# Factorization kernel: order of accumulating transfers, W loads, bias additions and x sums

## Chip, cores and metric

One NeuronCore of a Trainium2 chip runs the whole program. The metric is device time in microseconds (us); lower is better. A core has five engines that run side by side, each through its own program in order: TensorE (PE, with its weight loads listed as PEld), VectorE (DVE), ScalarE (ACT), GpSimd (POOL) and SyncE (SP). They meet through semaphores. DMA transfers are issued here by SP (loads, stores) and by GpSimd (transfers that add to their destination).

## The reference

`x` is 1024 x 512, `weight` is 64 embeddings x 512 x 512, all float32:

```python
out_lin = x @ lin_w.T + lin_b
xv = jnp.einsum('bf,efm->bem', x, weight)
zp = jnp.einsum('bf,efm->bem', jnp.square(x), jnp.square(weight))
interaction = 0.5 * jnp.sum(jnp.square(xv) - zp, axis=1)
return out_lin + interaction
```

The sum over embeddings of `zp` is `square(x)` times the sum of `square(W)`, one product. What stays is `x @ W` for 64 embeddings, squared and summed.

## The kernel before

**Tiling.** The embeddings go through in 16 groups of four (`q`). One group is a product of `x` with four matrices, done by Strassen's method in Winograd's form at two levels: 7 outer products (`i` of "1", "2", "6", "7", "5", "3", "4", in this order) of 7 inner products each, and each for two halves `j` of the rows. That is 98 products a group, each of a 128x128 operand with 128x512 columns. W is held in four tiles `WB[kk][v]`: `kk` is a half of the contraction, `v` a pair of embeddings; one tile is 1 MB.

**Operands.** The x operands of all 49 combinations are made once, at the start, into `xs` by `outer_x` and `inner_x` (L154 to L185: two outer and four inner sums for each outer product). The W operands are made in every group on GpSimd: `outer_t` (L380, sums of whole tiles into `T5`, `T6` or `WB[0][0]`) and `inner_t`, which makes three tiles for each outer product: `tp` (L391, 128x1024), `t6` (L393) and `t4` (L395, both 128x512). They feed the inner products "5" and "7", "6", and "4".

**Results.** Each pair (outer product, `j`) is a `unit` with three PSUM banks `x`, `v`, `y`. ScalarE copies `x` into `y` (L475), after which `y` is added to; VectorE combines the banks with earlier results into `z` tiles (L446, L457, L458, L467), GpSimd does `rest` (L472). When a quarter of the output is complete in `z`, ScalarE squares it in place (`squares`, L497), and `gather` (L506) adds it to the accumulators `acc[0]` (in the profile acc_69) or `acc[1]` (acc_70) in SBUF by an accumulating DMA on GpSimd's queue. A gather to the same part of an accumulator waits for the gather before it to land. The names "c", "a", "b" tell which third of the results a gather carries; "c" to r=1 and "a" go in four transfers of 512 KB, (j=0, u=0), (1, 0), (0, 1), (1, 1), the others in two of 1 MB.

**Squares of W.** `w_squares` (L510) squares two halves of W tiles into `w2_sb` on ScalarE (L515), then an accumulating DMA of 1 MB adds `w2_sb` to `w2_sum` (L522): four times a group. There is one `w2_sb`.

**Order.** Nothing is scheduled by a tool. Every step is put into a `Stream` with a number `t`; the steps are sorted by it and issued in this order, so `t` fixes only the order within each engine's program. It isn't a time at which something starts. One unit of `t` is about one product, and a group covers 98:

```python
for _, _, fn in sorted(self.items, key=lambda v: v[:2]):
    fn()
```

Units start at `g0 + 14*n + 7*j`, with `g0 = 98*q`, and their inner products "1", "5", "6", "2", "7", "3", "4" stand at +0, +2, +4, +6, +8, +10, +12. Consecutive units overlap, so the product at `t` is product number t - 3 of its group (counted from the 98*q-th product). For instance "4" of unit (1, j=0), at t = 12, is number 9 and reads `t4` of outer product "1"; "6" of unit (2, j=0), at 18, is number 15 and reads `t6` of "2"; "6" of unit (4, j=0), at 88, is number 85.

**What the change touches.** L354: places of the bias additions `add_bias` (L348, one 128x512 VectorE operation for each of eight accumulator parts, in groups 1 to 4). L538: order of the four W loads of the next group on SP's queue (L358). L543 to L557: places of `outer_t` and `inner_t`. L567 and L568: places of gathers. L580: place of the first W squares of a group; L521: how far their accumulating transfer stands behind them. L596: the x sums of outer product "7". L758: a sum of squared x (`last_sx`, L628) for the last product.

Of the kernel before, what the change touches and what calls it, by code (L numbers as in the profile page):

```python
# [28 lines left out]
def kernel(  # L29
# [31 lines left out]
    nc = tc.nc  # L61
# [45 lines left out]
    def xsl(i, o):  # L107
        return xs[:, SLOT[i], SLOT[o], :]

    st = Stream()  # L110
# [35 lines left out]
    def quarter(r, kk, n):  # L146

        w = slice(0, 3) if n is None else n
        for i, rk in BLOCK.items():
            if rk == (r, kk):  # L150
                return a21[i] if n == 3 else xs[:, SLOT[i], w, :]
        return A21[:, w, :]

    def outer_x(i, eng=nc.vector):  # L154
        if i in BLOCK:
            return []

        def put(n):
            w = slice(0, 3) if n is None else n

            def of(o):
                return a21[o] if n == 3 else xs[:, SLOT[o], w, :]

            def src(r, kk):
                return quarter(r, kk, n)

            if i == "5":
                eng.tensor_add(of(i), src(1, 0), src(1, 1))
            elif i == "6":
                eng.tensor_sub(of(i), of("5"), src(0, 0))  # L170
            elif i == "7":
                eng.tensor_sub(of(i), src(0, 0), src(1, 0))
            else:
                eng.tensor_sub(of(i), src(0, 1), of("6"))

        return [lambda: put(None), lambda: put(3)]

    def inner_x(i, eng=nc.vector):
        add, sub = eng.tensor_add, eng.tensor_sub
        return [  # L180
            lambda: add(xsl(i, "5"), a21[i], xsl(i, "4")),
            lambda: sub(xsl(i, "6"), xsl(i, "5"), xsl(i, "1")),
            lambda: sub(xsl(i, "7"), xsl(i, "1"), a21[i]),
            lambda: sub(xsl(i, "3"), xsl(i, "2"), xsl(i, "6")),
        ]  # L185
# [160 lines left out]
    def add_bias(r, j, s):  # L346
        o = acc[r][:, j, s]
        nc.vector.scalar_tensor_tensor(o, bias, 2.0, o, ALU.mult, ALU.add)  # L348
# [1 line left out]
    st.at(-1, lambda: nc.sync.dma_start(bias, lin_b.partition_broadcast(P)))  # L350

    for n in range(4):
        for r, t in enumerate((22.6, 36.6)):
            st.at(98 * (n + 1) + t, lambda r=r, n=n: add_bias(r, n // 2, n % 2))  # L354

    def load_w(q, kk, v):
        src = weight[4 * q + 2 * v : 4 * q + 2 * v + 2]
        nc.sync.dma_start(  # L358
            WB[kk][v], src.rearrange("u (p k) m -> p u k m", k=NK)[:, :, ts(kk, 2)]
        )  # L360
# [12 lines left out]
    def outer_t(i, u):  # L373
        a, b = {
            "5": (WB[0][1], WB[0][0]),
            "6": (WB[1][1], T5),
            "7": (WB[1][1], WB[0][1]),
            "4": (WB[1][0], T6),
        }[i]
        nc.gpsimd.tensor_sub(OUTER[i][:, u], a[:, u], b[:, u])  # L380
# [3 lines left out]
    def inner_t(q, i, n):  # L384

        b = OUTER[i]
        k = 2 if n == "tp" else 1
        t = tpool.tile([P, k, M], F32, tag=n, name=f"{n}_{q}_{i}")
        TI[q, i, n] = t
        if n == "tp":  # L390
            nc.gpsimd.tensor_sub(t, b[:, 1], b[:, :, 0])  # L391
        elif n == "t6":
            nc.gpsimd.tensor_sub(t[:, 0], b[:, 1, 1], TI[q, i, "tp"][:, 0])  # L393
        else:
            nc.gpsimd.tensor_sub(t[:, 0], b[:, 0, 1], TI[q, i, "t6"][:, 0])  # L395
# [96 lines left out]
    def squares(t, q, n, j, wait):  # L492
        z = place(q, n)
        for u in range(2):
            st.at(
                t + max(wait, 0.1) * u,
                lambda u=u: nc.scalar.activation(z[:, u, j], z[:, u, j], AF.Square),  # L497
            )
# [3 lines left out]
    def gather(t, q, n, r, j, u):  # L502
        def fn():
            z = place(q, n)[:, u]
            o, z = (acc[r], z) if j is None else (acc[r][:, j], z[:, j])
            nc.gpsimd.dma_start(o, z, accum_op=ALU.add)  # L506

        st.at(t, fn)

    def w_squares(t, q, v, u):  # L510
        first = q == v == u == 0

        def sq(kk):
            o = (w2_sum if first else w2_sb)[:, ts(kk, 2)]
            nc.scalar.activation(o, WB[kk][v][:, u], AF.Square)  # L515

        for kk in range(2):
            st.at(t + 0.1 * kk, lambda kk=kk: sq(kk))
        if not first:
            st.at(  # L520
                t + 5,  # L521
                lambda: nc.gpsimd.dma_start(w2_sum, w2_sb, accum_op=ALU.add),  # L522
            )

# [10 lines left out]
    for q in range(NQ):  # L535
        g0 = 98 * q
        last = q == NQ - 1
        for kk, v, t in ((1, 0, -41), (0, 1, -39), (0, 0, -37), (1, 1, -10)):  # L538
            if q:
                st.at(g0 + t, lambda q=q, kk=kk, v=v: load_w(q, kk, v))  # L540

        for i, t0, t1 in (
            ("5", -8, 2) if q else ("5", -11, -10.9),  # L543
            ("6", 14.2, 14.3) if q else ("6", 0.5, 0.6),
            ("7", 28.7, 28.8),
            ("4", 50, 53),
        ):
            for u, t in enumerate((t0, t1)):
                st.at(g0 + t, lambda i=i, u=u: outer_t(i, u))
        for i, *times in (  # L550
            ("1", -4.3, -0.6, 2.1) if q else ("1", -11.5, -11.4, -11.3),
            ("2", 6.4, 10.1, 10.2) if q else ("2", -5, -4.9, -4.8),
            ("6", 20.7, 20.8, 27),
            ("7", 34.4, 34.5, 39.7),
            ("5", 43.1, 43.2, 43.3),
            ("3", 57.9, 58, 61.7),
            ("4", 81, 81.1, 81.2),  # L557
        ):
            for n, t in zip(("tp", "t6", "t4"), times):
                st.at(g0 + t, lambda q=q, i=i, n=n: inner_t(q, i, n))  # L560
        for n, (i, (addend, dst)) in enumerate(UNITS.items()):
            for j in range(2):
                unit(g0 + 14 * n + 7 * j, q, i, j, addend, dst)

        for k, n, r, times in (
            (1, "c", 0, ((None, 38.8), (None, 52.9))),
            (4, "c", 1, ((0, 73), (0, 87), (1, 80), (1, 92.8))),  # L567
            (5, "a", 0, ((0, 88), (0, 99.5), (1, 96.5), (1, 107.2))),  # L568
            (6, "b", 1, ((None, 111.3), (None, 124.2))),
        ):  # L570
            for j in range(2):
                t = g0 + 14 * k + 7 * j + 14.6
                squares(t - (0.95 if last and n == "b" else 0), q, n, j, 4 * (k == 4))
            for m, (j, t) in enumerate(times):
                if not last or n == "c":
                    gather(g0 + t, q, n, r, j, m % 2)
        if q == 0:
            w_times = (-6, 14.8, 37, 56.6)
        else:
            w_times = (-15, 14.8, 37, 56.6)  # L580
        for n, t in enumerate(w_times):
            w_squares(g0 + t, q, n // 2, n % 2)
    for kk, v in ((0, 0), (1, 0), (0, 1), (1, 1)):
# [3 lines left out]
    for sums, t in (  # L587
# [5 lines left out]
    ):  # L593
        for n, fn in enumerate(sums):
            st.at(t + 0.1 * n, fn)
    for n, fn in enumerate(outer_x("7") + inner_x("7")):  # L596
        st.at(7.6 + 1.1 * n, fn)
    for n, fn in enumerate(outer_x("3", nc.gpsimd) + inner_x("3", nc.gpsimd)):
        st.at(36.9 + 0.1 * n, fn)

# [10 lines left out]
    def square_xq(r, kk):  # L613
        nc.scalar.activation(XQ[r][:, kk], XQ[r][:, kk], AF.Square)
# [7 lines left out]
    def last_sx(i):  # L622
        t = WB[0][0] if i in "56" else T5
        t = t.rearrange("p u l (n q) -> p u (l n) q", q=Q)
        SX[i] = t[:, "5673".index(i) % 2]
        a21, a22 = XQ[1][:, 0], XQ[1][:, 1]
        if i == "5":
            nc.gpsimd.tensor_add(SX[i], a21, a22)  # L628
        elif i == "6":
            nc.gpsimd.tensor_sub(SX[i], SX["5"], last_x("1"))  # L630
        elif i == "7":
            nc.gpsimd.tensor_sub(SX[i], last_x("1"), a21)
        else:
            nc.gpsimd.tensor_sub(SX[i], last_x("2"), SX["6"])
# [120 lines left out]
        st.at(g + t, lambda r=r: load_xq(r))  # L755
    for t, r, kk in ((-28, 1, 0), (-27.9, 1, 1), (-25, 0, 0), (-24.9, 0, 1)):
        st.at(g + t, lambda r=r, kk=kk: square_xq(r, kk))
    for i, t in zip("5673", (-24.1, -9.9, -9, -5)):  # L758
        st.at(g + t, lambda i=i: last_sx(i))
    for i, t in zip("5674", (-9.8, -9.7, -8.9, -4.9)):  # L760
        st.at(g + t, lambda i=i: last_tw(i))
# [71 lines left out]
```

## Time and profile before

| | us |
|---|---|
| runs: median of 3 (lowest to highest) | 1413.41 (1413.05 to 1416.66) |
| the profiled execution | 1413.1 |
| its span, first to last instruction | 1411.2 |
| busy: TensorE | 1402.8 |
| busy: GpSimd | 1244.5 |
| busy: VectorE | 883.1 |
| busy: ScalarE | 623.2 |
| one group of 98 products, groups 1 to 14 (first weight load to first weight load in the trace) | 84.1 to 85.2 |

So 1.9 us of the profiled execution lie outside its span, and it is 0.3 us below the median. The granted TensorE clock is 1.00 throughout. TensorE's row must be read with care: matmuls are pipelined and their ends are modelled, so short stalls don't show in it. The weight loads (PEld) start evenly, two for each product; where two starts lie further apart, TensorE stood still.

### The profile page before, as it was taken

What the parts mean: (1) busy time and instruction counts of PE and PEld (TensorE: products, weight loads), DVE (VectorE), ACT (ScalarE), POOL (GpSimd) and SP (SyncE); (2) the same over time, 40 slices, a digit from 0 to 9 for tenths busy, and PEclk for the clock granted to TensorE, in tenths of its full rate; (3) what the DMA queues carried; (4) which work ended last, traced back from release to release, by engine and by line L of the source; (5) the groups of instructions that cost most, each with busy time, mean ns of one, the idle gap of its engine ahead of it and who ended that gap; (6) DMA issues with size and microseconds to landing.
All of it is one profiled execution on the core that took longest, in us unless ns stands there. A gap on an engine that the chain in (4) does not pass through costs nothing.

```text
span 1411.2 us, 11148 instructions
## 1 busy us (share of the span) xinstructions
PE 1402.8 (99%) x3340; PEld 633.7 (45%) x3340; DVE 883.1 (63%) x1277; ACT 623.2 (44%) x824; POOL 1244.5 (88%) x806
## 2 busy tenths in 40 slices
PE   9999999999999999999999999999999999999999
PEld 5444444444444444444444444444444444444446
DVE  6765657657576565656656566565656656566565
ACT  3344353453534444352453535444352453535443
POOL 7788989888898888989998899888989989899894
PEclk9999999999999999999999999999999999999999
DMA  5299898999989899898999989889898989989876
GB/s 216 52 216 208 190 212 167 225 189 220 189 177 223 167 220 208 191 212 162 235 181 225 192 182 219 172 213 202 192 209 170 230 178 229 188 181 224 169 179 142
DMA packets 58108, 273.63 MB, mean 194 GB/s; under 512 B 5440, under 2 KB 8000, under 8 KB 41792
## 3 DMA queue, kind: packets, MB, share of 16 engines
q0 software_dynamic: 36432, 198.20, 71.6%
q1 hardware_dynamic: 21328, 74.19, 15.1%
q10 hardware_dynamic: 288, 0.52, 0.1%
q8 instruction: 27, 0.44, 0.1%
q14 instruction: 33, 0.27, 0.0%
HBM read 72.61 MB, written 2.10 MB: 53 GB/s over the span
## 4 chain that ended last, share of the span: by engine, by line
PE 80%; POOL 9%; DMA 8%; issue 2%; DVE 1%; ACT 0%; POOLq 0%; ACTq 0%; DVEq 0%
PE y L421 33%; PE v L421 22%; PE x L421 21%; DMA acc<-z 5%; DMA w<-weight 3%; POOL t L380 2%; POOL tp L391 2%; POOL z L472 1%; POOL t L393 1%; PE lin L216 1%; POOL acc L506 1%; POOL t L395 1%; PE y_last L660 1%; POOL w_sum L522 1%; PE x_last L660 0%
## 5 line engine op out<-in xcount | busy, mean ns | idle before, releaser
L421 PE MATMUL y<-t,xs 128*128 128x512 f32 x896 | 422.0, 593 | 3.3 <-DVE z L467 1.8
L475 ACT COPY y<-x 128x512 f32<-128x512 f32 x224 | 127.8, 570 | 573.7 <-PE x L421 573.5
L467 DVE TENSOR_TENSOR z<-y,s 128x512 f32<-128x512 f32 x192 | 132.8, 692 | 237.1 <-PE y L421 236.0
L497 ACT ACTIVATE z<-z 128x1024 f32<-128x1024 f32 x256 | 260.2, 1054 | 22.7 <-POOL z L472 20.2
L421 PEld LDWEIGHTS y<-t,xs 128*128 128x128 f32 x896 | 169.5, 190 | 219.7 <-issue 209.8
L506 POOL DMA_DIRECT2D acc<-z x190 | 196.4, 1056 | 68.9 <-DMA acc<-z 33.2
L421 PE MATMUL x<-w,xs 128*128 128x512 f32 x512 | 248.4, 592 | 0.0
L421 PE MATMUL y<-tp,xs 128*128 128x512 f32 x448 | 229.3, 593 | 0.7 <-DVE s L446 0.6
L421 PE MATMUL v<-tp,xs 128*128 128x512 f32 x448 | 228.9, 592 | 0.4 <-POOL tp L391 0.4
L472 POOL TENSOR_TENSOR z<-z,s 128x1024 f32<-128x1024 f32 x64 | 149.9, 2364 | 46.3 <-DVE s L467 46.3
L421 PE MATMUL x<-t,xs 128*128 128x512 f32 x384 | 188.3, 592 | 0.0
L391 POOL TENSOR_TENSOR tp<-w 128x1024 f32<-128x1024 f32 x64 | 175.5, 2743 | 4.1 <-PE y L421 2.9
L467 DVE TENSOR_TENSOR z<-v,s 128x512 f32<-128x512 f32 x192 | 132.7, 691 | 71.0 <-PE v L421 69.2
L458 DVE TENSOR_TENSOR z<-y,z 128x512 f32<-128x512 f32 x192 | 132.4, 690 | 55.8 <-PE y L421 55.6
L380 POOL TENSOR_TENSOR t<-w,t 128x1024 f32<-128x1024 f32 x64 | 159.3, 2567 | 0.0
L458 DVE TENSOR_TENSOR z<-x,z 128x512 f32<-128x512 f32 x192 | 132.3, 689 | 35.8 <-PE x L421 34.3
L421 PEld LDWEIGHTS x<-w,xs 128*128 128x128 f32 x512 | 97.3, 190 | 122.0 <-issue 121.3
L515 ACT ACTIVATE w_sb<-w 128x1024 f32<-128x1024 f32 x126 | 126.0, 1050 | 28.0 <-DMA w<-weight 23.5
L391 POOL TENSOR_TENSOR tp<-t 128x1024 f32<-128x1024 f32 x48 | 137.1, 2855 | 0.0
L421 PEld LDWEIGHTS y<-tp,xs 128*128 128x128 f32 x448 | 84.7, 190 | 109.0 <-issue 103.8
L421 PEld LDWEIGHTS v<-tp,xs 128*128 128x128 f32 x448 | 85.0, 190 | 107.9 <-issue 103.4
L421 PE MATMUL v<-w,xs 128*128 128x512 f32 x256 | 130.7, 592 | 0.0
(113 smaller groups left out, 1448.3 us busy)
## 6 DMA issues: line engine op xcount, KB each, us to landing
w<-weight SPq DMA_DIRECT2D x64, 1024.0 KB, 11.2
acc<-z POOLq DMA_DIRECT2D x128, 512.0 KB, 8.6
w_sum<-w_sb POOLq DMA_DIRECT2D x63, 1024.0 KB, 12.3
acc<-z POOLq DMA_DIRECT2D x62, 1024.0 KB, 7.6
w<-x SPq DMA_DIRECT2D x2, 1024.0 KB, 10.3
out<-z SPq DMA_DIRECT2D x7, 256.0 KB, 2.3
xs<-x SPq DMA_DIRECT2D x2, 384.0 KB, 7.0
t<-lin_wT ACTq DMA_DIRECT2D x2, 256.0 KB, 3.8
```

The costliest lines, as they stand in the source:

```text
L216: nc.tensor.matmul(LIN[n], quarter(0, kk, (0, 1, 3, 2)[2 * s + l])[:, ts(j, P)], lw_sb[:, 2 * kk + l, :], start=(kk == 0 and l == 0), stop ...
L380: nc.gpsimd.tensor_sub(OUTER[i][:, u], a[:, u], b[:, u])
L391: nc.gpsimd.tensor_sub(t, b[:, 1], b[:, :, 0])
L393: nc.gpsimd.tensor_sub(t[:, 0], b[:, 1, 1], TI[q, i, "tp"][:, 0])
L421: nc.tensor.matmul(d[bank], xsl(i, o)[:, ts(j, P)], operand_b(q, i, o), start=start, stop=True, skip_group_check=True,)
L458: nc.vector.tensor_add(zblk(q, dst, j, b), d[bank], zblk(q, addend, j, b))
L467: nc.vector.tensor_add(s if both else zblk(q, dst, j, b), d[bank], s)
L472: nc.gpsimd.tensor_add(place(q, n)[:, 1, j], place(q, src)[:, 1, j], d["s"])
L475: st.at(t0 + 0.5, lambda: nc.scalar.copy(d["y"], d["x"]))
L497: lambda u=u: nc.scalar.activation(z[:, u, j], z[:, u, j], AF.Square),
L506: nc.gpsimd.dma_start(o, z, accum_op=ALU.add)
L515: nc.scalar.activation(o, WB[kk][v][:, u], AF.Square)
```

## The change

Four kinds of edits:

- two bias additions a group (groups 1 to 4) stand 5 places later;
- on SP, W tile (0, 0) is loaded second and (0, 1) third, instead of the reverse; the load of (1, 1) gets another number;
- the first W squares of a group stand 4.2 places earlier, and with them the accumulating transfer to `w2_sum`; a smaller distance (3.2 instead of 5) is written for t < 0; some gathers and W sums stand at other places;
- the x sums of outer product "7" are made by GpSimd before its first `outer_t("6")`, not by VectorE among the first units; `last_sx("5")` stands 10.1 places later.

No operation is added or removed.

```diff
     for n in range(4):
-        for r, t in enumerate((22.6, 36.6)):
+        for r, t in enumerate((27.6, 41.6)):
             st.at(98 * (n + 1) + t, lambda r=r, n=n: add_bias(r, n // 2, n % 2))
...
             st.at(
-                t + 5,
+                t + (3.2 if t < 0 else 5),
                 lambda: nc.gpsimd.dma_start(w2_sum, w2_sb, accum_op=ALU.add),
             )
...
-        for kk, v, t in ((1, 0, -41), (0, 1, -39), (0, 0, -37), (1, 1, -10)):
+        for kk, v, t in ((1, 0, -41), (0, 0, -37.5), (0, 1, -37), (1, 1, -3)):
...
-            ("5", -8, 2) if q else ("5", -11, -10.9),
+            ("5", -9.9, 2) if q else ("5", -11, -10.9),
...
-            ("1", -4.3, -0.6, 2.1) if q else ("1", -11.5, -11.4, -11.3),
-            ("2", 6.4, 10.1, 10.2) if q else ("2", -5, -4.9, -4.8),
+            ("1", -6.4, -1.4, 2.1) if q else ("1", -11.5, -11.4, -11.3),
+            ("2", 6.4, 6.5, 10.2) if q else ("2", -5, -4.9, -4.8),
...
-            ("4", 81, 81.1, 81.2),
+            ("4", 81, 82.1, 84.1),
...
-            (4, "c", 1, ((0, 73), (0, 87), (1, 80), (1, 92.8))),
-            (5, "a", 0, ((0, 88), (0, 99.5), (1, 96.5), (1, 107.2))),
+            (4, "c", 1, ((0, 73), (0, 84), (1, 80), (1, 91.5))),
+            (5, "a", 0, ((0, 88), (0, 99.5), (1, 96.5), (1, 110.3))),
...
-            w_times = (-15, 14.8, 37, 56.6)
+            w_times = (-19.2, 14.8, 37, 56.6)
...
-    for n, fn in enumerate(outer_x("7") + inner_x("7")):
-        st.at(7.6 + 1.1 * n, fn)
-    for n, fn in enumerate(outer_x("3", nc.gpsimd) + inner_x("3", nc.gpsimd)):
-        st.at(36.9 + 0.1 * n, fn)
+    for i, t in (("7", -4.7), ("3", 36.9)):
+        for n, fn in enumerate(outer_x(i, nc.gpsimd) + inner_x(i, nc.gpsimd)):
+            st.at(t + 0.1 * n, fn)
...
-    for i, t in zip("5673", (-24.1, -9.9, -9, -5)):
+    for i, t in zip("5673", (-14, -9.9, -9, -5)):
         st.at(g + t, lambda i=i: last_sx(i))
```

The order on GpSimd around the start of a group becomes, with the order of before under it:

```
after:  tp4 t6_4 WSUM c(0,1) t4_4 a(0,0) outer5 c(1,1) tp1 a(1,0) t6_1 a(0,1) outer5 t4_1 tp2 t6_2 t4_2 a(1,1) b outer6
before: tp4 t6_4 t4_4 c(0,1) a(0,0) WSUM outer5 c(1,1) tp1 a(1,0) t6_1 a(0,1) outer5 t4_1 tp2 a(1,1) t6_2 t4_2 b outer6
```

Here `t6_2` is the tile `t6` of outer product "2", `a(0,1)` the gather of "a" for j=0, u=1, and WSUM the accumulating transfer to `w2_sum`. On ScalarE the two W squares now stand between the two squares of "c" for j=1, instead of behind both.

## The prediction, made before the run

> **What bounds the kernel now.** I read the page first, for the engines and queues.
>
> ```profile
> PE 1402.8 (99%) x3340; PEld 633.7 (45%) x3340; DVE 883.1 (63%) x1277; ACT 623.2 (44%) x824; POOL 1244.5 (88%) x806
> ...
> q0 software_dynamic: 36432, 198.20, 71.6%
> q1 hardware_dynamic: 21328, 74.19, 15.1%
> ```
>
> TensorE is the bound, and the DMA engines (87% over both queues) and GpSimd (88%) are close behind: a reordering can win only what TensorE loses in stalls, and it must not run into the other two. So I went through the weight loads in order of time. Two loads start 0.43 us apart when nothing stalls. From 26 us on, 20 distances exceed 0.5 us; what they have above 0.43 each sums to 12.98 us. Five kinds make it up, and each is shown once.
>
> Kind 1, the bias. The timelines of weight loads and of VectorE, group 1:
>
> ```profile
> 151.14 0.30 PEld L421 LDWEIGHTS y<-tp,xs 128*128 128x128 f32 x2 [1.03 <-DVE s L446]
> ...
> 148.06 1.24 DVE L348 SCALAR_TENSOR_TENSOR acc<-bias,acc 128x512 f32<-128x512 f32 x1 [1.54 <-DMA acc<-z]
> 149.22 0.68 DVE L446 TENSOR_TENSOR s<-v,z 128x512 f32<-128x512 f32 x1
> ```
>
> The second bias addition of a group waits 1.54 us for a gather to land, and the results behind it come late. Four groups have bias, and four distances of this kind exist (1.22, 1.22, 1.07, 1.21): 3.00 us.
>
> Kind 2, W squares. The ScalarE timeline and the weight load it held, group 7:
>
> ```profile
> 694.12 2.00 ACT L515 ACTIVATE w_sb<-w 128x1024 f32<-128x1024 f32 x2 [3.30 <-DMA w<-weight]
> 696.03 0.58 ACT L475 COPY y<-x 128x512 f32<-128x512 f32 x1
> ...
> 696.72 0.30 PEld L421 LDWEIGHTS y<-t,xs 128*128 128x128 f32 x2 [1.38 <-issue]
> ```
>
> The squares wait for W(0,0), the third load in the row; the copy behind them, which product 85 needs, is late. Distances 0.53, 1.57, 1.08, 0.74, 0.90: 2.67 us.
>
> Kind 3, t6 behind a gather. GpSimd and the weight load, group 11:
>
> ```profile
> 971.61 0.88 POOL L506 DMA_DIRECT2D acc<-z  x1 [3.35 <-ACT y L475]
> 972.22 1.58 POOL L393 TENSOR_TENSOR t<-w,tp 128x512 f32<-128x512 f32 x1
> ...
> 973.84 0.30 PEld L421 LDWEIGHTS y<-t,xs 128*128 128x128 f32 x2 [1.30 <-POOL t L393]
> ```
>
> The gather a(1,1) waits for a(1,0), which landed at 971.1 (ScalarE, named as releaser, had long been done). Four such (0.55, 1.49, 1.21, 1.27) and three small ones that follow them: 3.08 us.
>
> Kind 4, the start. VectorE and the weight load:
>
> ```profile
> 32.74 2.46 DVE L181 TENSOR_TENSOR xs<-z,xs 128x256 f32<-128x256 f32 x1
> 35.23 2.46 DVE L182 TENSOR_TENSOR xs<-xs 128x256 f32<-128x256 f32 x1
> ...
> 38.28 0.95 DVE L172 TENSOR_TENSOR xs<-xs,z 128x768 f32<-128x768 f32 x1
> 39.15 0.68 DVE L467 TENSOR_TENSOR z<-y,s 128x512 f32<-128x512 f32 x1
> ...
> 39.95 0.30 PEld L421 LDWEIGHTS y<-t,xs 128*128 128x128 f32 x2 [2.56 <-issue]
> ```
>
> Product 9 of group 0 waits for L467, which stands behind x sums: 2.75 - 0.43 = 2.32 us. Kind 5, once, at the end: tp4 of the last group (1370.76, distance 1.38) is late by 0.95 us behind L628. The last two distances (31.94 us: 0.45; 675.30 us: 0.51) are behind other ScalarE copies, and I leave them.
>
> **What the Trainium skill says.** "SBUF — State Buffer", section "SBUF: two separate sides": VectorE operations with two SBUF inputs and GpSimd take one port pair by an exclusive lock, held for the whole instruction. The trace agrees: L182 takes 2.46 us beside GpSimd's 128x1024 operations and 0.41 alone (41.14 us). "DMA: Bandwidth & Descriptors", section "Issuing engines are not separate DMA queues": transfers of all engines interleave on the same 16 DMA engines. Its section "Two DMAs through the same engine are not ordered" asks the issuer to wait for the first transfer's semaphore; so a gather holds up all of GpSimd's program, as in kind 3.
>
> **Part by part.**
>
> Bias. At 41.6 it comes behind the L458 of unit (6, j=1), about 34.8 us into the group; the gather it needs landed 32.0 us into group 1 and, after the change, at about 32.5 to 33. VectorE idles about 1.0 us before its next L467, and the addition takes 0.97 to 1.24 us (one of eight 2.2, beside a long GpSimd operation); the L467 has some 1.5 us until TensorE needs its bank. Gain 3.0; bounds 2 to 3.
>
> Loads of W. SP issues strictly in order, with nothing else between, so -10 to -3 for (1,1) changes nothing. W(0,0) becomes second; second loads landed at products 73.5 to 78.5, third ones at 79 to 83. The squares follow ScalarE's square at 76 to 77 and end by 80.5, before the copy at 82. W(0,1), now third, is read by outer5 at about 88. Its landing up to 83 is hidden by that. Kind 2 goes: gain 2.7, bounds 2 to 2.7.
>
> The distance 3.2 is never used: `t` there includes g0, and the only negative one, in group 0, is the first, which has no transfer. WSUM stands at -14.2, behind t6_4.
>
> t6_2, t4_2 ahead of a(1,1). Gain 3.1 where they come in time; see below.
>
> x sums of "7". GpSimd gets 1.81 us (L174, same shape) and 5 x 0.73 us: 5.5 us, from 32.4 to 37.9. Then outer6 ends at 42.7. What is behind, WSUM, had waited until 45.69 for ScalarE (8.28 us idle), so this is hidden; TensorE's first stall there being gone, ScalarE comes some 2.3 us earlier, at 43.4, still later. VectorE's L181 to L184 now meet short GpSimd operations instead of two long ones: ends 34.5, 35.2, 35.9, 36.6; L467 follows, ready at 37.3, needed at 37.6. Gain 2.3, bounds 1.4 (only the 0.95 of L172 removed, and a little) to 2.3.
>
> `last_sx("5")`: tp4 comes 2.4 us earlier. It now delays t4_4, ready at 1373.4 and needed at 1379. Gain 0.95.
>
> Sum of gains: 3.0 + 2.7 + 3.1 + 2.3 + 0.95 = 12.0.
>
> **The new wait.** WSUM now enters the queue ahead of c(0,1) and a(0,0). Take group 2, which starts at 200.61. GpSimd:
>
> ```profile
> 200.41 0.88 POOL L506 DMA_DIRECT2D acc<-z  x1 [0.58 <-DMA acc<-z]
> 201.02 2.66 POOL L380 TENSOR_TENSOR t<-w,w 128x1024 f32<-128x1024 f32 x1
> 203.34 1.56 POOL L395 TENSOR_TENSOR t<-w,t 128x512 f32<-128x512 f32 x1
> 204.57 2.64 POOL L391 TENSOR_TENSOR tp<-w 128x1024 f32<-128x1024 f32 x1
> ```
>
> At 200.41 a(0,1) was released by the landing of a(0,0) at 200.12. After the change a(0,0) has 1 MB more before it: 4.9 us (a(0,0) to WSUM, 200.12 to 205.02). The queue starts earlier, since WSUM is issued when t6_4 ends (188.1), not when t4_4 ends (189.44): 1.35 us, in which the windows of the trace show the DMA engines idle (after the window and its length: busy PE, PEld, DVE, ACT, POOL; then clock, DMA share, GB/s):
>
> ```profile
> 187.50:190.50 3.00, 3.00 (x8) 1.33 (x7) 1.81 (x3) 2.77 (x4) 2.92 (x4) 1.00 0.04 7
> 190.50:200.20 9.70, 9.70 (x24) 4.20 (x23) 6.50 (x10) 3.17 (x5) 9.33 (x7) 1.00 1.03 238
> ```
>
> So a(0,0) lands at 200.12 + 4.9 - 1.35 = 203.7. GpSimd gets there at the same time as before, since the operations ahead are the same. It waits 3.6 us more. Behind it: outer5 (not urgent), t4_1 and tp2. t4_1 ended 4.78 us after the landing (200.12 to 204.90), so at 208.45, 7.85 us into the group. Product 9 needs it at 9 x 0.858 = 7.72 us, less a small delivery: a stall of about 0.2. tp2 (10.2, needed at 11.2) and t6_2 (11.5, needed at 12.9) come in time, and a(1,1) then waits for nothing. So this wait takes up all the slack that t4_1 had, 2.8 us, and a little more, in 15 groups. Landings of a(0,0) before, against the group's start, were -0.5 in groups 1 to 4 and up to +1.3 later (partly through kind 2). From below: nothing, if WSUM fills the idle time better; from above: 1.1 us a group, if all groups land as late as 11 and 14. I take 0.4: 15 x 0.4 = 6 us.
>
> Forecast: 1411.2 - 12.0 + 6.0 = 1405.2 span, + 1.9 outside = 1407.
>
> **Rivals.** (a) The new wait costs nothing: 1413.1 - 12 = 1401. For it: the idle DMA time; against: t4_1 has no slack left by the sum. (b) It takes most of the gain: 0.6 to 0.95 us a group, 9 to 14 us; 1410 to 1415. For it: the spread of landings, and that without stalls a group gives the DMA engines 0.5 to 0.8 us less. (c) Slower: the same mechanism beyond its turning point. Each 0.1 us by which a(0,0) lands later than 203.5 in group 2's time costs 1.5 us; at 0.8 a group the gain of 12 is gone, at 1.1 the kernel is 0.3% slower. That needs landings 3.9 us into the group, 0.8 above my sum; then 1418 to 1422. Group 11's c(0,1) took 9.5 us to land beside a W load instead of 6.2, so it isn't excluded.
>
> **Chances.** Forecast (1403.5 to 1409) 0.42, (a) 0.18, (b) 0.24, (c) 0.16. About 0.3%, 4.2 us, is what a measurement can tell from no change. Faster by more: 0.42 + 0.18 = 0.60; within: 0.24; slower: 0.16. The range takes in (a), the forecast and (b): 1400 to 1416.
>
> **What would show it.** Right: no distance behind L348, L515 or t6_2 any more; product 9 of group 0 on time; GpSimd idle some 3 to 4 us before a(0,1), with a small stall at product 9 of each group, released by L395. Wrong: that stall above 0.8 us, or new ones at tp6 or tp4, whose slack was about 1 us; or kind 2 still there because W(0,0) lands as late as before.

## The result, and the profile after

| | us |
|---|---|
| before, median of 6 runs (lowest to highest) | 1414.06 (1412.49 to 1417.99) |
| changed kernel, median of 6 runs | 1423.93 (1422.90 to 1425.68) |
| ratio, 95% interval | 1.0067, 1.0051 to 1.0083 |
| span of the profiled executions | 1411.2 before, 1422.1 after |

The change makes the kernel 0.7% slower. The page of the changed kernel, busy time of each engine and the shares of the chain that ended last:

```profile
PE 1407.7 (99%) x3340; PEld 636.5 (45%) x3340; DVE 893.6 (63%) x1271; ACT 620.8 (44%) x824; POOL 1248.8 (88%) x812
...
PE 94%; DMA 2%; issue 1%; POOL 1%; DVE 1%; ACT 0%; POOLq 0%
```

TensorE is still the bound and no operation was added, but VectorE is busy 10.5 us longer. The view of waits (engine and line, what it waited for; us in total, times, longest) names who held a weight load:

```profile
PEld y L421 <- DVE z L467: 12.9, 4, 3.5
```

Four weight loads waited over 3 us each for L467 of VectorE, and four groups have bias. To place these waits I cut the span at each group's first weight load:

| us | before | changed |
|---|---|---|
| first weight load of group 0, at | 29.98 | 31.49 |
| group 0 | 86.03 | 84.04 |
| groups 1, 2, 3, 4 | 84.59, 84.58, 84.44, 84.58 | 88.40, 88.37, 86.69, 88.87 |
| groups 5 to 10, sum | 505.72 | 504.72 |
| groups 11, 12, 13, 14 | 85.18, 84.58, 84.12, 84.79 | 85.04, 84.20, 84.12, 84.12 |
| group 15, to its last weight load of L421 | 87.77 | 87.14 |
| the rest | 24.91 | 24.90 |

98 products at 0.858 us are 84.1 us, so 84.12 is a group without a stall. No other group got longer; the four with bias lost 14.1 us together. I don't count the 1.5 us at the start to the change: the start lies between 29.98 and 31.49 in the ten kernels of this study, one profiled execution each, without a pattern.

Inside group 1, VectorE and then GpSimd (start, length, instruction, idle time before it and its releaser):

```profile
149.63 0.69 DVE L458 TENSOR_TENSOR z<-x,z 128x512 f32<-128x512 f32 x1 [0.17 <-PE x L421]
150.24 5.31 DVE L348 SCALAR_TENSOR_TENSOR acc<-bias,acc 128x512 f32<-128x512 f32 x1
155.47 0.68 DVE L467 TENSOR_TENSOR z<-y,s 128x512 f32<-128x512 f32 x1
```

```profile
149.62 0.87 POOL L506 DMA_DIRECT2D acc<-z  x1
150.22 1.56 POOL L395 TENSOR_TENSOR t<-w,t 128x512 f32<-128x512 f32 x1
151.44 1.18 POOL L522 DMA_DIRECT2D w_sum<-w_sb  x1
152.04 2.94 POOL L391 TENSOR_TENSOR tp<-t 128x1024 f32<-128x1024 f32 x1
155.07 1.61 POOL L393 TENSOR_TENSOR t<-t,tp 128x512 f32<-128x512 f32 x1
```

The bias addition waits for no semaphore and takes 5.31 us. It comes at 150.24, while GpSimd still issues a gather (149.62 to 150.49). It runs past the end of t4_7 at 151.78 and ends at 155.55, 0.57 us after tp5 has ended at 154.98. So it is held for the length of two GpSimd operations. That it is held at the port pair which the prediction names is a reading at this point; the third experiment tests it. The same row before and after (shortest, median and longest in ns, then the first and last start):

```profile
L348 DVE SCALAR_TENSOR_TENSOR acc<-bias,acc x8: 966/1188/2204, 134.4 to 400.7; 128x512 f32<-128x512 f32 x8
```

```profile
L348 DVE SCALAR_TENSOR_TENSOR acc<-bias,acc x8: 1371/3518/5667, 138.3 to 414.0; 128x512 f32<-128x512 f32 x8
```

The median lies between two clusters: the four first additions of a group take 1.37 to 1.75 us, the four second ones 5.28 to 5.67. The weight loads of the changed kernel behind the addition of group 1, and after it those of group 3:

```profile
152.86 0.19 PEld L421 LDWEIGHTS y<-t,xs 128*128 128x128 f32 x1 [0.24 <-issue]
156.20 0.30 PEld L421 LDWEIGHTS y<-t,xs 128*128 128x128 f32 x2 [3.15 <-DVE z L467]
...
158.05 0.34 PEld L421 LDWEIGHTS x<-w,xs 128*128 128x128 f32 x1 [0.52 <-issue]
158.90 0.34 PEld L421 LDWEIGHTS x<-w,xs 128*128 128x128 f32 x1 [0.52 <-issue]
...
332.96 0.30 PEld L421 LDWEIGHTS y<-t,xs 128*128 128x128 f32 x2 [3.14 <-DVE z L467]
333.50 0.19 PEld L421 LDWEIGHTS x<-w,xs 128*128 128x128 f32 x1 [0.24 <-issue]
333.93 0.19 PEld L421 LDWEIGHTS x<-w,xs 128*128 128x128 f32 x1 [0.24 <-issue]
```

Both stalls are equally long, but in group 1 the loads behind it come 0.85 us apart instead of 0.43. Windows of the same two stretches show why (window and length; busy PE, PEld, DVE, ACT, POOL; clock, DMA share, GB/s):

```profile
153.00:156.20 3.20, 0.88 (x3) 0.05 (x1) 3.20 (x3) 0.00 (x0) 3.12 (x2) 1.00 1.00 200
156.20:158.00 1.80, 1.80 (x3) 0.82 (x4) 1.80 (x4) 0.00 (x0) 0.93 (x2) 0.76 0.96 196
158.00:160.60 2.60, 2.60 (x5) 1.03 (x4) 1.23 (x2) 0.00 (x0) 2.60 (x2) 0.51 1.19 243
160.60:165.00 4.40, 4.40 (x12) 2.01 (x11) 2.76 (x4) 0.57 (x1) 3.70 (x3) 1.00 0.63 127
333.00:337.00 4.00, 4.00 (x10) 1.85 (x11) 3.19 (x6) 0.57 (x1) 3.20 (x3) 1.00 1.00 205
```

The granted clock falls to half for 3.4 us (157.1 to 160.5) after TensorE has idled, and then comes back. Half of 3.4 us is 1.7 us of lost work, and that is the difference between group 1 and group 3: 88.40 - 86.69 = 1.7 us. The Trainium skill, "TensorE: Matmul & The Clock Gate", section "Part 1: The HAM clock gate (the "warmup" mystery)", has half rate after an idle window of about 3.4 us, whose phase runs freely. A free phase agrees with the traces: idle times of the weight loads of 3.12 and 3.15 us, and of 3.24 us in the run with the places alone, were followed by it, while 3.14 us, and 3.22 us in that run, were not. The page's length does not: these are shorter than 3.4 us, and here the measurement decides.

### The profile page after: what moved, and what is told of

Same layout as the page of the kernel before. It is cut to its first block, busy times and chain, and to the rows that moved or that the text cites. A ratio compares the mean times of both kernels' runs of the same rounds, so it can differ in the third digit from the quotient of the medians.

```text
span 1422.1 us, 11166 instructions
## 1 busy us (share of the span) xinstructions
PE 1407.7 (99%) x3340; PEld 636.5 (45%) x3340; DVE 893.6 (63%) x1271; ACT 620.8 (44%) x824; POOL 1248.8 (88%) x812
## 4 chain that ended last, share of the span: by engine, by line
PE 94%; DMA 2%; issue 1%; POOL 1%; DVE 1%; ACT 0%; POOLq 0%
PE y L421 39%; PE x L421 26%; PE v L421 25%; DMA acc<-z 2%; PE lin L216 1%; PE y_last L659 1%; DVE acc L348 1%; PE v_last L659 0%; PE x_last L659 0%; POOL t L380 0%; PE y_lin L271 0%; DMA t<-lin_wT 0%; POOL t L395 0%; PE v_lin L271 0%; PE x_lin L271 0%
## 5 line engine op out<-in xcount | busy, mean ns | idle before, releaser
L421 PE MATMUL y<-t,xs 128*128 128x512 f32 x896 | 424.0, 594 | 10.3 <-DVE z L467 9.6
L467 DVE TENSOR_TENSOR z<-y,s 128x512 f32<-128x512 f32 x192 | 132.7, 691 | 238.0 <-PE y L421 238.0
L421 PEld LDWEIGHTS y<-t,xs 128*128 128x128 f32 x896 | 169.7, 190 | 226.7 <-issue 202.8
L506 POOL DMA_DIRECT2D acc<-z x190 | 213.2, 1153 | 64.3 <-DMA acc<-z 62.7
L421 PE MATMUL x<-w,xs 128*128 128x512 f32 x512 | 252.0, 600 | 0.0
L421 PE MATMUL y<-tp,xs 128*128 128x512 f32 x448 | 229.1, 593 | 0.0
L421 PE MATMUL v<-tp,xs 128*128 128x512 f32 x448 | 228.8, 592 | 0.0
L421 PE MATMUL x<-t,xs 128*128 128x512 f32 x384 | 188.3, 592 | 0.0
L467 DVE TENSOR_TENSOR z<-v,s 128x512 f32<-128x512 f32 x192 | 132.8, 691 | 72.2 <-PE v L421 70.6
L380 POOL TENSOR_TENSOR t<-w,t 128x1024 f32<-128x1024 f32 x64 | 164.1, 2725 | 0.0
L421 PEld LDWEIGHTS x<-w,xs 128*128 128x128 f32 x512 | 98.4, 192 | 123.8 <-issue 123.5
L421 PEld LDWEIGHTS y<-tp,xs 128*128 128x128 f32 x448 | 85.6, 191 | 107.8 <-issue 107.8
L421 PEld LDWEIGHTS v<-tp,xs 128*128 128x128 f32 x448 | 85.1, 190 | 107.3 <-issue 104.2
L421 PE MATMUL v<-w,xs 128*128 128x512 f32 x256 | 130.7, 592 | 0.0
L446 DVE TENSOR_TENSOR s<-v,z 128x512 f32<-128x512 f32 x160 | 110.6, 691 | 27.8 <-PE v L421 27.1
```

Source lines behind the costliest of these rows:

```text
L421: nc.tensor.matmul(d[bank], xsl(i, o)[:, ts(j, P)], operand_b(q, i, o), start=start, stop=True, skip_group_check=True,)
L446: nc.vector.tensor_add(o, d[bank], zblk(q, addend, j, b))
L467: nc.vector.tensor_add(s if both else zblk(q, dst, j, b), d[bank], s)
```

## The experiments

My theory from these lines has two parts. The port theory: both inputs of the addition are in SBUF, and so GpSimd's operations hold it up, here two of them. Theory A says why it is two: the place 41.6 puts the second addition into the moment in which GpSimd issues the gather c(0,0); an addition that arrives then is passed over at the end of the next GpSimd operation and held to the end of the one after. The rivals: the loss comes with the other edits, whose wait for a(0,0) or whose transfers press on the stretch; or the addition is slow for another reason than GpSimd's operations, by its place in VectorE's order or because of the gathers that write the same accumulators.

**The old places (e1).** The changed kernel with the bias additions where they were:

```diff
-        for r, t in enumerate((27.6, 41.6)):
+        for r, t in enumerate((22.6, 36.6)):
```

> The changed kernel with the two bias additions at their places of before (22.6 and 36.6). Port theory (at 41.6 the addition meets two GpSimd operations one after the other and holds up VectorE, TensorE stops and its clock drops for a moment): groups 1 to 4 fall from 88.4 us to about 84.6 to 85.5, granted clock back to 1.00, time 1410 to 1413, some 0.2% under before. Rival (the loss comes from the other edits, such as the x sums or the earlier transfer to w2_sum, and the bias addition only shows it): groups 1 to 4 stay above 87 us, time above 1420.

Measured: 1411.44 us (1411.08 to 1412.45), ratio to before 0.9976, 0.9965 to 0.9987. Span 1409.6, clock 1.00. Of its VectorE timeline, group 1:

```profile
148.63 0.81 DVE L348 SCALAR_TENSOR_TENSOR acc<-bias,acc 128x512 f32<-128x512 f32 x1 [3.37 <-DMA acc<-z]
149.35 0.68 DVE L446 TENSOR_TENSOR s<-v,z 128x512 f32<-128x512 f32 x1
```

The loss is gone with one pair of numbers, 12.5 us on the median, so the other edits together are a gain. The old place has its own price: the gather lands later after the change, the addition waits 1.94 to 3.37 us for it, and groups 1 to 4 take 85.99, 84.66, 84.64 and 85.35 us, the first of them more than the 85.5 expected.

**The places alone (e2).** The kernel before with nothing but 27.6 and 41.6:

```diff
-        for r, t in enumerate((22.6, 36.6)):
+        for r, t in enumerate((27.6, 41.6)):
```

> The kernel before with the bias additions alone moved to 27.6 and 41.6. Port theory: the second addition takes about 5.3 us again, groups 1 to 4 rise from 84.5 to about 88.4 us, time 1426 to 1430, slower than the changed kernel. Rival (the place is harmless without the other edits): additions of 1 to 2 us, groups 1 to 4 near 84.1, time 1411 to 1413.

Measured: 1426.45 us (1424.52 to 1428.77), ratio 1.0077, 1.0058 to 1.0096. VectorE in group 1:

```profile
151.15 5.19 DVE L348 SCALAR_TENSOR_TENSOR acc<-bias,acc 128x512 f32<-128x512 f32 x1
```

The second additions take 5.19 to 5.40 us, groups 1 to 4 86.59, 88.37, 88.49 and 86.78. Two groups stay below the 88.4 expected: their stalls, of 3.03 and 3.22 us, were not followed by the half clock. One edit alone makes the kernel as slow as all of them together, so the first rival falls: nothing else of the change is needed for the loss.

**The port (e3).** The changed kernel with the addition at the same place, but one SBUF operand taken from a PSUM bank; it adds 0 times that bank, so the bias is left out:

```diff
-        nc.vector.scalar_tensor_tensor(o, bias, 2.0, o, ALU.mult, ALU.add)
+        nc.vector.scalar_tensor_tensor(o, LAST["x"], 0.0, o, ALU.mult, ALU.add)
```

> The changed kernel; at the same places the addition takes a PSUM bank times 0 in place of the bias tile, so it has one SBUF input and the bias is left out of the result. Port theory (two SBUF inputs are what collides): 0.7 us each, never waiting for GpSimd, groups 1 to 4 at 84.1 to 84.3 us, clock 1.00, time 1406 to 1409. Rival (the wait belongs to the accumulator or its gather, or to the place in VectorE's order): still some 5 us each, groups 1 to 4 above 87 us.

Measured: 1407.83 us (1407.42 to 1408.28), ratio 0.9945, 0.9930 to 0.9960. The row of its eight operations (two lines were added above, so L350 is L348):

```profile
L350 DVE SCALAR_TENSOR_TENSOR acc<-x,acc x8: 680/680/681, 138.1 to 402.7; 128x512 f32<-128x512 f32 x8
```

All eight take 0.68 us, beside the same GpSimd operations and gathers and with the same output. The second rival falls too: it is neither the place in VectorE's queue nor the accumulator, but the second SBUF input. The Trainium skill, "SBUF — State Buffer", section "SBUF: two separate sides", says that a VectorE operation with both inputs in SBUF contends with a GpSimd operation that reads SBUF; the trace agrees, with 5.3 us for two SBUF inputs against 0.68 for one.

**A free place (e4).** The changed kernel with each addition behind an L467 at whose time GpSimd waits for VectorE; the eight additions are spread over eight groups:

```diff
-        for r, t in enumerate((27.6, 41.6)):
-            st.at(98 * (n + 1) + t, lambda r=r, n=n: add_bias(r, n // 2, n % 2))
+        for r in range(2):
+            st.at(
+                98 * (2 * n + r + 1) + 65,
+                lambda r=r, n=n: add_bias(r, n // 2, n % 2),
+            )
```

> The changed kernel with the eight bias additions at t = 65 of groups 1 to 8, one a group, where GpSimd waits for VectorE and both idle for 1 us. Port theory: about 0.7 us each, all groups from 1 to 10 at 84.1 to 84.2 us, time 1406 to 1409, faster than both kernels. Rival (an addition costs TensorE time wherever it stands): groups 1 to 8 at 84.5 or more, time 1410 or more.

Measured: 1407.29 us (1406.75 to 1407.74), ratio 0.9940, 0.9923 to 0.9957. VectorE, then GpSimd, of its timeline (three lines were added above, so L470 is the L467 of the other kernels):

```profile
169.36 0.69 DVE L470 TENSOR_TENSOR s<-y,s 128x512 f32<-128x512 f32 x1 [0.43 <-PE y L424]
169.97 0.68 DVE L348 SCALAR_TENSOR_TENSOR acc<-bias,acc 128x512 f32<-128x512 f32 x1
```

```profile
167.65 1.56 POOL L398 TENSOR_TENSOR t<-w,t 128x512 f32<-128x512 f32 x1
171.92 2.35 POOL L475 TENSOR_TENSOR z<-z,s 128x1024 f32<-128x1024 f32 x1 [2.70 <-DVE s L470]
```

With GpSimd idle from 169.21 to 171.92 the addition with both operands in SBUF takes 0.68 us too. So, with e3, it takes both: two inputs in SBUF and a working GpSimd. Groups 1 to 3 take 84.12 us; group 4 takes 84.44, by a wait at product 9 that belongs to the other edits (see "The new wait" below). The median is 16.6 us under the changed kernel's: the bias additions cost TensorE nothing at this place.

**The free place in the kernel before (e5).** The same edit of the places, made there:

> The kernel before with the eight bias additions at t = 65 of groups 1 to 8, and nothing else changed. It parts the bias from the other edits. If groups are the right measure of a stall, the bias cost before only 4 x 0.45 us and this saves 1.5 to 2 us: groups 1 to 4 at 84.1, time some 1412 to 1413, no difference clear of noise. If the distances between weight loads are the right measure, as in the prediction, it saves 3.0 us.

Measured: 1412.86 us (1410.10 to 1414.64, 12 runs), ratio 0.9989, 0.9978 to 0.9999. Groups 1 to 4 take 84.12 each, so the bias stalls are gone, worth 0.47 + 0.46 + 0.32 + 0.46 = 1.7 us. In the execution profiled, group 7 took 88.60 us instead of 85.12: the stall of kind 2, which this edit leaves in, was 3.36 us long there, and the loads behind it came 0.85 us apart. So the median is less clear than the groups.

**Behind the operation instead of beside the issue (e6).** In the changed kernel the gather c(0,0) is put behind t4_7, so that the second addition arrives while t4_7 runs:

```diff
-            (1, "c", 0, ((None, 38.8), (None, 52.9))),
+            (1, "c", 0, ((None, 39.75), (None, 52.9))),
```

> The changed kernel, bias at 27.6 and 41.6, with only the first gather of c to acc[0] moved on GpSimd from in front of t4 of outer product 7 (38.8) to behind it (39.75). Nothing moves on VectorE. Theory A (an addition that arrives while GpSimd issues a DMA misses the next operation's end as well; one that arrives during an operation gets in at its end): the second addition arrives during t4 and takes 1.2 to 1.6 us, groups 1 to 4 at 84.2 to 84.6, time 1407 to 1410. Theory B (it is held over two operations at this place whatever GpSimd does before): again about 5 us, groups 1 to 4 at 87 to 88.5, time above 1420.

Measured: 1411.28 us (1410.50 to 1412.71, 20 runs), ratio 0.9975, 0.9968 to 0.9982. VectorE and GpSimd, group 1:

```profile
149.07 1.33 DVE L348 SCALAR_TENSOR_TENSOR acc<-bias,acc 128x512 f32<-128x512 f32 x1
150.33 0.68 DVE L467 TENSOR_TENSOR z<-y,s 128x512 f32<-128x512 f32 x1
```

```profile
148.59 1.27 POOL L395 TENSOR_TENSOR t<-w,t 128x512 f32<-128x512 f32 x1
149.80 0.87 POOL L506 DMA_DIRECT2D acc<-z  x1
150.38 1.18 POOL L522 DMA_DIRECT2D w_sum<-w_sb  x1
150.94 3.00 POOL L391 TENSOR_TENSOR tp<-t 128x1024 f32<-128x1024 f32 x1
```

The addition comes to the same L395 0.48 us after its start and is served at its end, 0.54 us later. The four second additions take 1.33 to 1.70 us, groups 1 to 3 84.12 and group 4 84.52, as theory A has it; neither the addition nor its place in VectorE's order was touched. But the edit changed two things: when the addition arrives, and what follows t4_7. With both issues behind t4_7, 1.08 us pass before tp5 starts (149.86 to 150.94), where it was 0.26 us (151.78 to 152.04).

The time missed the 1407 to 1410 expected; it is some 4 us above e4's. ScalarE, near the end:

```profile
1359.93 2.00 ACT L613 ACTIVATE w<-w 128x1024 f32<-128x1024 f32 x2 [5.11 <-DMA w<-x]
```

It waits 5.11 us for the last load of x (0.93 in the changed kernel); group 15 takes 89.33 instead of 87.14, and the rest 26.49 instead of 24.90. That is 3.8 us. Part of the delay can be followed: counted from the start of group 15, the moved gather is issued 1.35 us later (35.42 instead of 34.07) and lands 1.3 us later, and the transfers behind it follow, a W sum 1.4, a gather 1.6 and the first load of x 1.9 us later. The last load of x lands 4.3 us later (65.71 instead of 61.44); where the rest of that comes from stays open.

**Is it the second issue? (e8)** In the first runs two issues stand around t4_7, the gather's and the W sum's. Here the W sum's goes behind tp5, so that tp5 follows t4_7 directly:

```diff
-                t + (3.2 if t < 0 else 5),
+                t + (6.11 if v == 1 and u == 0 else 5),
```

> The changed kernel, bias at 27.6 and 41.6, with the third transfer to w2_sum of every group moved on GpSimd from between t4 of outer product 7 and tp of outer product 5 to behind that tp. The gather in front of t4 stays, so the second addition still arrives while GpSimd issues a DMA. Theory A (an arrival during a DMA issue misses the end of the next operation, whatever follows): 4.5 to 5 us each, groups 1 to 4 above 86.5. Theory C (it missed the end of t4 because the second DMA issue overlapped this end): it gets in between t4 and tp, 1.9 to 2.3 us each, groups 1 to 4 under 85.5.

Measured, a single run: 1414.87 us, beside 1417.38 of the kernel before on the same chip. VectorE and GpSimd, group 1:

```profile
149.61 4.35 DVE L348 SCALAR_TENSOR_TENSOR acc<-bias,acc 128x512 f32<-128x512 f32 x1
```

```profile
148.93 0.88 POOL L506 DMA_DIRECT2D acc<-z  x1
149.54 1.57 POOL L395 TENSOR_TENSOR t<-w,t 128x512 f32<-128x512 f32 x1
150.77 2.63 POOL L391 TENSOR_TENSOR tp<-t 128x1024 f32<-128x1024 f32 x1
153.06 1.18 POOL L522 DMA_DIRECT2D w_sum<-w_sb  x1
```

The addition is still passed over at t4_7's end (151.11) and ends 0.56 us after tp5's (153.40). All four take 4.35 to 4.75 us, groups 1 to 4 85.75, 85.78, 85.82 and 86.49, a little under what theory A expected (4.5 to 5 us, above 86.5) and far from theory C's 1.9 to 2.3. So the second issue isn't what it takes; it only adds 0.9 us. What e6 and e8 leave are two differences: the moment of arrival, during an operation in one and during the gather's issue in the other; and the operation behind t4_7. That is tp5, which doesn't need t4_7's result, and it follows without a break in e8 and after 1.08 us in e6.

The trace of before speaks on the second. Near its start a VectorE sum with both inputs in SBUF, on a smaller tile, meets a GpSimd operation behind which one follows that doesn't need its result, without a break. VectorE, then GpSimd:

```profile
20.80 1.48 DVE L184 TENSOR_TENSOR xs<-xs 128x256 f32<-128x256 f32 x1
```

```profile
20.68 1.33 POOL L395 TENSOR_TENSOR t<-w,t 128x512 f32<-128x512 f32 x1
21.97 4.86 POOL L380 TENSOR_TENSOR t<-w,w 128x1024 f32<-128x1024 f32 x2
```

The sum arrives 0.12 us after the start of L395 and ends 0.27 us after its end (22.01), so it did not wait for L380. That speaks for the moment of arrival, though it isn't the same operation, and no run parts the two differences for the addition itself. Nor is any issue enough: in groups 1 to 3 of e1 the first addition arrived 0.04 to 0.07 us after the issue of a W sum had begun, but behind an operation that was still running, and it was served at that operation's end (1.2 us in all). All twelve additions that were passed over (four each in the changed kernel, e2 and e8) came during the issue of a gather that stands ahead of the next operation. Why that operation then goes first, these runs don't tell.

**The best of both (e7).** e4, with the smaller distance (3.2) given to the first accumulating transfer of a group, where the change wrote it for t < 0:

```diff
-                t + (3.2 if t < 0 else 5),
+                t + (3.2 if u == v == 0 else 5),
```

> The changed kernel with the bias at t = 65 of groups 1 to 8, and with the distance 3.2 in effect for the first W squares of every group, so that their transfer to w2_sum stands in front of t6 of outer product 4. Theory: a(0,0) lands about 1.3 us earlier, 1.6 us into the group, t4 of outer product 1 ends at about 6.4 us and the stalls at product 9 in groups 4, 11 and 12 (0.1 to 0.9 us) go: 0.5 to 1.5 us faster than the run with the bias alone moved, 1405.5 to 1407. Rival: t6 of outer product 4, now 0.9 us later with 0.5 us of slack left, stalls TensorE instead: no faster or slower.

Measured: 1406.17 us (1406.05 to 1406.65), ratio 0.9944, 0.9928 to 0.9961. Groups 1 to 14 take 84.12 us each: no stall is left in them. It is the lowest time of the study, 0.56% below the kernel before; its interval overlaps e4's, so the W sum's share is read from the group lengths (0.3 us less in each of groups 4 and 11), not from the medians.

## Why the prediction was wrong

**Bias: the step that failed.** "VectorE idles about 1.0 us before its next L467, and the addition takes 0.97 to 1.24 us (one of eight 2.2, beside a long GpSimd operation) ... Gain 3.0; bounds 2 to 3." The place was right: 34.8 us into the group predicted, 150.24 - 115.53 = 34.7 measured. What failed is the cost of the addition: its duration was taken along from the old place. Even there it was misread: three of the eight took 2.20, not one. All eight of these additions had arrived while a GpSimd operation was running. What would be running at the new place could be read in the trace of before; its GpSimd timeline, 34.8 us into group 1 (which starts at 116.01, so at 150.8):

```profile
150.37 0.87 POOL L506 DMA_DIRECT2D acc<-z  x1
150.98 1.57 POOL L395 TENSOR_TENSOR t<-w,t 128x512 f32<-128x512 f32 x1
152.20 1.19 POOL L522 DMA_DIRECT2D w_sum<-w_sb  x1
152.81 2.97 POOL L391 TENSOR_TENSOR tp<-t 128x1024 f32<-128x1024 f32 x1
```

The place falls into the issue and ahead of two operations. No addition of before stood so, and its price was unknown: the end of tp5 (5.0 us on) belonged into the bounds as a loss, but the bounds had no loss at all. Measured: the addition takes 5.28 to 5.67 us there, and groups 1 to 4 take 15.8 us above 4 x 84.12, some 10.7 by the stalls and 5.1 by the half clock behind three of them (1.7 each). 1.7 of it had been there before, so 14.1 are lost.

**Loads of W** held: kind 2 is gone from the changed kernel. (In e6 a stall at product 85 came back once, 0.7 us in group 7, behind W squares that had waited 3.92 us for their load.) **t6_2 ahead of a(1,1)** held: no stall behind it is left. **x sums** held: group 0 fell by 2.0 us (predicted 2.3). **last_sx** held in direction: group 15 fell by 0.63 (predicted 0.95).

**The gains were over-measured.** The prediction added what the distances have above 0.43 us. But the weight load behind such a gap follows the held one 0.11 us later (the 0.30 us "x2" rows hold two), and so up to 0.32 us of every gap is made up at once. By group lengths the kernel before had 2.0 (group 0) + 1.7 (bias) + 1.0 (7) + 1.1 (11) + 0.5 (12) + 0.7 (14) + 0.6 (15) = 7.6 us to give, not 12.0.

**The new wait** was foreseen and came, but was priced too high. GpSimd of the changed kernel, group 2 (which starts at 203.93) and group 11 (at 972.55), and the weight load of product 9 in group 11:

```profile
207.06 0.87 POOL L506 DMA_DIRECT2D acc<-z  x1 [4.01 <-DMA acc<-z]
...
209.98 1.57 POOL L395 TENSOR_TENSOR t<-w,t 128x512 f32<-128x512 f32 x1
...
976.97 0.88 POOL L506 DMA_DIRECT2D acc<-z  x1 [4.83 <-DMA acc<-z]
...
979.90 1.57 POOL L395 TENSOR_TENSOR t<-w,t 128x512 f32<-128x512 f32 x1
```

```profile
981.52 0.30 PEld L421 LDWEIGHTS y<-t,xs 128*128 128x128 f32 x2 [1.48 <-POOL t L395]
```

a(0,0) lands 2.8 us into group 2 (predicted 3.1), GpSimd waits 4.01 us (0.58 + 3.6 = 4.2 predicted) and t4_1 ends 7.6 us in (7.85), just in time; in group 11 it ends 8.9 us in and costs 0.9. Over all groups the wait costs 1.4 us in e3 (0.9 in group 11, 0.3 in group 4, 0.1 each in 8 and 12) and 0.7 us in e4, where 15 x 0.4 = 6 were taken. The step was right in its mechanism and its term too large.

So e3 and e4, the change with a harmless addition, came out at 1407.8 and 1407.3, beside the 1407 forecast. That is luck and no support for the sum: 12.0 and 6 were both too large, and the errors nearly cancel (12.0 - 6 = 6.0; 7.6 - 1.4 = 6.2). And the slower rival had the sign but not the cause: it put the loss on a(0,0), and a(0,0) cost some 1.4 us.

## What to carry to other kernels

Place a VectorE operation with both inputs in SBUF by what GpSimd does when it arrives, not by VectorE's free time alone: read GpSimd's timeline at the new place, and where an issue and then long operations stand there, put the end of the second one into the bounds. A duration measured at one place isn't the duration at another. Measure stalls by the length of a stretch with a fixed amount of work, not by adding up gaps, and look for a drop of the clock behind an idle time of some 3 us (the shortest that had one here was 3.12 us).

## What the hardware did that I hadn't expected

- An addition that came while a GpSimd operation ran was served about 0.55 us after its end (1.3 to 1.8 us in all in e6). One that came while GpSimd issued a gather ahead of its next operation was passed over once and served behind the second operation: 5.19 to 5.67 us with another issue between the two, 4.35 to 4.75 without. In group 4 of the changed kernel the addition came at 414.02, 0.35 us before t4_7 began, and still went behind it and tp5 (5.67 us). The section of "SBUF — State Buffer" named above says that the one that starts first gets the port pair for its whole instruction. By the recorded starts the addition was ahead of both operations and got it behind both; the issue of the gather had begun 0.26 us before it.
- After 3.14 us of idle time TensorE went on at full clock (group 3), after 3.15 us at half (group 1): one such stall costs 2.6 or 4.3 us.
